# A graph network on one core: in the account of a hand-planned order, the transposed attention squares land later

## The chip, the core and the metric

The kernel runs on one core of a Trainium2 chip. The metric is device time in microseconds for one launch. A profiled execution also gives the span from the first to the last instruction, and a trace of all engines: TensorE (PE, its weight loads PEld), VectorE (DVE), ScalarE (ACT), GpSimd (POOL) and SyncE (SP), which issues the DMAs here.

## What is computed

There are 128 graphs of 128 nodes with 256 features, and a dense adjacency matrix for each. Everything is float32.

```python
# layer 0: gated graph network, three steps with shared GRU weights
h = relu(layernorm(x))
for i in range(3):
    m = h @ weight[i]
    aggr = einsum('bst,bsd->btd', A, m)          # A = adj != 0
    h = gru_cell(aggr, h, w_ih, w_hh, b_ih, b_hh)
x = x + h
# layer 1: graph attention
h = relu(layernorm(x))
Wh = h @ W.T
s1, s2 = Wh @ a1, Wh @ a2
e = leaky_relu(s1[:, :, None] + s2[:, None, :], 0.2)
att = softmax(where(adj == 0, -inf, e), axis=-1)
x = x + einsum('bij,bjo->bio', att, Wh)
```

## The kernel before

**Tiling.** Four graphs form a group (`G = 4`), so there are 32 groups (`NG`). Each group goes through three GRU steps and then through an epilogue, which is the attention layer. The steps of several groups are interleaved by a fixed list, `plan`: 96 steps, and each group's three steps stand apart so that other groups' steps lie between them.

**A GRU step** (`gru_step`) has two phases. Each phase is seven block products in the manner of Strassen's method, and each product is 6 matmuls of 128x256 (L690) into the PSUM tiles `u`, `m7`, `c1` and `c2`; in the profile they are `u`, `m` and `c`. ScalarE and VectorE copy and add these between the products (L710 to L725) and make the gates (L743 to L785). The neighbours' sums for a later step come from the gather `pa` (L598), 16 matmuls of 128x128.

**The epilogue** (`epilogue`) of a group does the following. The state is turned to rows and added to the input (`x1`). The rows are normalised (`norm_scales`, `norm_apply`) into `h_b`. The two score vectors are made by `scalar_tensor_tensor` with a sum (L922). The squares `e`, 128x128 for each graph, are filled from a broadcast score line, masked, reduced and passed through the exponential (L958 to L979). Then the squares have to be transposed. For groups 0 to 28 that is `squares_by_blocks`: VectorE transposes 32x32 blocks into `prT` (L571), and `by_way_of_dram` moves the blocks to their places, with four DMAs to a DRAM tile (`z_e<-prT`) and four back (`e<-z_e`). For the last three groups (`late`) TensorE transposes them through PSUM (`pp`, L988, and `prT`, L992). Then come the attention product `pq<-e,h_b` (`gathered`, L598, 16 matmuls), two copies to `hs` on ScalarE (L1019), the product with W in `po` (L1027), the last addition on VectorE (L1036) and one DMA to the output. The last group's epilogue is cut in two halves of two graphs each.

**PSUM.** `misc` has three banks. `pa` and `pq` take two of them at once, and so do the row transposes of the late groups (`pr_o`, L489) where they handle four graphs; `po`, `pp` and `ps` take one each.

**The order.** The order of instructions on every engine is decided while the program is built. The class `Order` keeps an account of time: `free` holds when each engine is next free, and `rooms` when each buffer is. Each piece of work is a generator that yields what it needs: an engine, a length, the time at which its inputs are ready and perhaps a room. It gets back the time at which the account has it done. `HOP` (0.2) is added to every ready time, and a DMA is taken to have landed `LAND` (2.5) after its issue. A task has a rank: the next step's inputs have 0, state updates 0.5, prologues 1 and epilogues 2. The account only sorts instructions into the queues. On the chip each instruction waits for its own semaphores, whatever the account said.

A gate product counts for 1.3 on TensorE. After each product two things happen: `fill` places work of the other engines up to the product's end, and `matmuls` puts other TensorE work behind it, if the account has it ready by then:

```python
        def matmuls(self, most):
            end = self.free[PE] + most
            ...
                    if engine != PE or self.free[PE] >= end:
                        continue
                    if self.begin(PE, *needs) <= self.free[PE] + 0.05:
                        self.issue(task)
```

So `pq` enters TensorE's queue at the end of the first product at which the account has the squares landed and two `misc` banks free. In `by_way_of_dram` that landing is counted from the end of the block transpose: four issues of 0.67, `LAND`, four issues of 0.42, `LAND`, and whatever else the account has on SyncE.

All DMAs are issued by SyncE in that one order (the helper `dma`, L60). An issue that has to wait there holds up those behind it.

Of the kernel before, what the change touches and what calls it, by code (L numbers as in the profile page):

```python
# [15 lines left out]
D = 256  # L16
C = D // P
G = 4
# [9 lines left out]
def preln_gnn_kernel(  # L28
# [14 lines left out]
    nc = tc.nc  # L43
    B = x.shape[0]
    NG = B // G
# [11 lines left out]
    put = on_pe  # L57
# [107 lines left out]
    PE, ACT, DVE, DVE2, POOL, SP = "PE", "ACT", "DVE", "DVE2", "POOL", "SP"  # L165
# [125 lines left out]
    order = Order()  # L291
# [185 lines left out]
            put(nc.scalar.copy(hT[:, c, :], pt))  # L477
        return hT, t

    def to_rows(hT, ready, name, pairs=range(G // 2)):  # L480

        banks = []
        t = yield PE, 0.44 * len(pairs), ready, "misc", len(pairs)
        for half in pairs:
            pt = order.open("misc", f"pr_{name}_{half}").rearrange("p (k d) -> p k d", d=D)
            for k in range(2):
                for c in range(C):
                    n = half * 2 + k
                    put(nc.tensor.transpose(  # L489
                        pt[:, k, c * P : (c + 1) * P], hT[:, c, n * P : (n + 1) * P], ident  # L490
                    ))
            banks.append(pt)
        return banks, t
# [6 lines left out]
    def by_way_of_dram(tmp, to, n, ready, name, room=None):  # L500

        z = None
        for i in range(Q):
            t = yield SP, SMALL, ready
            if z is None:
                z = dram.tile([32, Q * n, Q, 32], F32, tag=f"z{n}", name=f"z_{name}", bufs=4)
            dma(z[:, :, i, :], tmp[i * 32 : (i + 1) * 32])
        order.close(f"tq_{name}" if n > G else f"prT_{name[:-2]}", t + LAND)
        ready = t + LAND
        rows_ = z.rearrange("r (q n) i a -> q r (n i a)", q=Q)  # L510
        to_ = None
        for q in range(Q):
            t = yield (SP, 0.42, ready) if to_ is not None else (SP, 0.42, ready, room)
            if to_ is None:
                to_ = to()
            dma(to_[q * 32 : (q + 1) * 32], rows_[q])
        return t + LAND
# [49 lines left out]
    def squares_by_blocks(e, prT, ready, name):  # L567

        t = yield DVE, 0.63, ready
        tmp = prT.rearrange("p k s -> p (k s)").rearrange("p (q k a) -> p q k a", q=Q, a=32)  # L570
        put(nc.vector.transpose(  # L571
            tmp.rearrange("p q k a -> p k q a"), e.rearrange("p k (q a) -> p k q a", q=Q)
        ))
        return (yield from by_way_of_dram(
            tmp.rearrange("p q k a -> p (q k) a"), lambda: e.rearrange("p k s -> p (k s)"),
            G, t, f"{name}_e",
        ))

    def rows(s, ready, name):

        banks, ready = yield from to_rows(s.hT, ready, name)
        h = None
        for half, pt in enumerate(banks):
            t = yield (ACT, 0.57, ready) if half else (ACT, 0.57, ready, "h")
            order.close(f"pr_{name}_{half}", t)
            if h is None:
                h = order.open("h", f"h_{name}")
            put(nc.scalar.copy(h[:, half * 2 : half * 2 + 2, :], pt))
        return h, t
# [48 lines left out]
    def state(s, o, old, new, v, z, ready):  # L638

        n = v[:, o, :]  # L640
        t = yield ACT, 0.66, ready
        put(nc.scalar.activation(n, n, AF.Tanh, bias=bih[:, 2 * C + o : 2 * C + o + 1], scale=1.0))  # L642
        s.halves.append(t)
        if len(s.halves) == C:
            n, new_, z_ = flat(v), flat(new), flat(z)
            t = yield DVE2, 1.22, max(s.halves)
            put(nc.vector.tensor_tensor(new_, flat(old), n, ALU.subtract))
            t = yield DVE2, 1.22, t - HOP
            put(nc.vector.scalar_tensor_tensor(new_, z_, 1.0, new_, ALU.add, ALU.mult))
            t = yield DVE2, 1.22, t - HOP  # L650
            put(nc.vector.scalar_tensor_tensor(new_, new_, 0.5, n, ALU.mult, ALU.add))
            s.halves.append(t)
            s.hT, s.aT = new, None
            s.l += 1
            if s.l < NL:
                s.hT_ready = max(s.halves)
                if s.by_blocks():
                    s.rows = order.add(1, state_rows(s))
                if s.due:
                    s.task = order.add(0, inputs(s, s.hT_ready))  # L660
            else:

                pairs = range(G // 2)
                for p in [pairs] if s.g < NG - 1 else [pairs[:1], pairs[1:]]:
                    order.add(2, epilogue(s, p, max(s.halves)))

    def gru_step(s, last):

# [134 lines left out]
    banks = dict.fromkeys(("u", "c1_0", "c1_1", "c2"), 0.0)  # L803
# [66 lines left out]
            "p n t -> p (n t)"  # L870
        ).rearrange("p (k s) -> p k s", s=P)

    def epilogue(s, pairs, ready):

        g = s.g
        graphs = range(2 * pairs[0], 2 * pairs[-1] + 2)
        n = len(graphs)
        part = slice(graphs[0], graphs[-1] + 1)
        cols = slice(part.start * P, part.stop * P)
        name = f"{g}_{pairs[0]}"  # L880
        bank_t, row_t, graph_t = 0.57 * n / G + 0.02, 0.62 * n / G + 0.02, 0.11 * n

        late, h = g >= NG - 3, None

        end = g >= NG - 2
        e_room, hs_room = (None, None) if end else ("e", "hs")
        if late:
            banks, ready = yield from to_rows(s.hT, ready, f"{name}_o", pairs)
        else:
            h, ready = yield from to_rows_by_blocks(s.hT, ready, f"b{name}")  # L890
            s.kept.append(h)
            if g < NG - XT:
                yield from load_x1(s)
                ready = max(ready, s.x1_ready)
        x1 = s.x1
        for half in pairs:
            t = yield (DVE if late else DVE2), 0.62, ready
            k2 = slice(half * 2, half * 2 + 2)
            if late:
                order.close(f"pr_{name}_o_{half}", t)  # L900
                put(nc.vector.tensor_add(x1[:, k2, :], x1[:, k2, :], banks[half - pairs[0]]))
            else:
                put(nc.vector.tensor_add(x1[:, k2, :], x1[:, k2, :], h[:, k2, :]))
        rstd, nb, t = yield from norm_scales(x1, graphs, t - HOP, f"b{name}")
        h, t = yield from norm_apply(
            x1, graphs, rstd, nb, t, f"b{name}", s.kept, "tq" if end else "h"
        )

        v = small.tile([P, 2, G], F32, tag="s", name=f"s_{name}")
        one, two = v[:, 0, :], v[:, 1, :] if late else score_tiles[g % 2][:, 0:G]  # L910
        ready = t
        for i in (1, 0):
            for k in graphs:
                first = not late and s.prT is None
                t = yield (DVE2, 0.53, ready, "prT") if first else (DVE2, 0.53, ready)
                if s.prT is None and late:
                    s.prT = io.tile([P, G, P], F32, tag="at", name=f"prT_{g}", bufs=AT)
                if s.prT is None:
                    s.prT = order.open("prT", f"prT_{g}")

                unused = s.prT[:, part.start : part.start + 2, :].rearrange("p k s -> p (k s)")
                put(nc.vector.scalar_tensor_tensor(  # L922
                    unused, h[:, k, :], 1.0, wa[:, i, :], ALU.mult, ALU.mult,
                    accum_out=(one, two)[i][:, k : k + 1],
                ))
# [8 lines left out]
        else:  # L934
# [4 lines left out]
            ready, line = t, None  # L939
# [62 lines left out]
        ))  # L1002

        banks, ready = yield from gathered(h, prT, t, f"pq_{name}", graphs)
        final = pairs[-1] + 1 == G // 2
        if final:
            order.close(f"h_b{g}_0", ready)
        if final and not end:
# [9 lines left out]
            hs = s.hs  # L1018
            put(nc.scalar.copy(hs[:, c, cols], pq[:, cols]))  # L1019
        ready = t  # L1020
        for half in pairs:
            t = yield PE, 1.73, ready, "misc"
            po = order.open("misc", f"po_{g}_{half}").rearrange("p (k d) -> p k d", d=D)
            for j in range(2):
                k = half * 2 + j
                for c in range(C):
                    put(nc.tensor.matmul(  # L1027
                        po[:, j, :], hs[:, c, k * P : (k + 1) * P], gwt[:, c, :],
                        start=(c == 0), stop=(c == C - 1),
                    ))  # L1030
            if final and half == pairs[-1] and not end:
                order.close(f"hs_{g}", t)
            for j in range(2):
                k = half * 2 + j
                t2 = yield DVE, 0.4, t
                put(nc.vector.scalar_tensor_tensor(  # L1036
                    x1[:, k, :], po[:, j, :], rs[:, k : k + 1], x1[:, k, :], ALU.mult, ALU.add
                ))
            order.close(f"po_{g}_{half}", t2)
        t = yield SP, 0.45, t2  # L1040
        ks = slice(g * G + part.start, g * G + part.stop)
        dma(out[ks].rearrange("b t d -> t b d"), x1[:, part, :])
# [140 lines left out]
```

## Time and profile before

| | |
|---|---|
| median of 3 runs | 2139.47 us (2136.89 to 2141.38) |
| the profiled execution's own time | 2138.47 us |
| its span | 2136.7 us |
| granted TensorE clock, mean | 0.999 |
| busy: PE, PEld | 2119.0 us (99%), 1879.0 us (88%) |
| busy: DVE, ACT, POOL | 1724.6 us (81%), 1302.4 us (61%), 105.9 us (5%) |
| moved by the SyncE queue | 209.87 MB |
| DMA issues `z_e<-prT`, `e<-z_e` | 116 each, 64 KB each |

A busy share is an average over the span. Matmuls are pipelined and their ends are modelled, so consecutive matmuls overlap in the trace; what counts is when the next one starts. "PE pq L598 <- DMA e<-z_e" means that TensorE's instruction at line 598 that writes `pq` waited for the DMA from `z_e` into `e`.

### The profile page before, as it was taken

Reading aid. Unit: us, or ns where it says so; the run is one execution under the profiler, and the core shown is the slowest. Engines: PE = TensorE matmul, PEld = TensorE weight load, DVE = VectorE, ACT = ScalarE, POOL = GpSimd, SP = SyncE. Lnnn points to the kernel's source line nnn. Section 1 sums busy time; section 2 is a strip of 40 time slices with the busy share of each in tenths; the row PEclk is TensorE's granted clock in tenths of the full one; section 3 lists DMA queues with packets and bytes.
Section 4 is the critical chain, followed back from the end, with each engine's and each line's share of the span. In section 5 each row is a group of like instructions: output and inputs, shape, how many; then the busy total and the mean of one; then the engine's idle time right before and its main releaser. Section 6 shows DMA issues by size and latency. Waiting matters only on the chain.

```text
span 2136.7 us, 32121 instructions
## 1 busy us (share of the span) xinstructions
PE 2119.0 (99%) x10763; PEld 1879.0 (88%) x10763; DVE 1724.6 (81%) x3763; ACT 1302.4 (61%) x2855; POOL 105.9 (5%) x204
## 2 busy tenths in 40 slices
PE   9999999999999999999999999999999999999997
PEld 7888888888888888888888888888888888888886
DVE  7777888788888888888888788888878887887777
ACT  6556566566666666665666566556656665665665
POOL 2000000000000000000000000000000000000000
PEclk9999999999999999999999999999999999999999
DMA  5333454444554273544445453734445354443301
GB/s 158 64 85 81 88 118 93 110 102 92 128 110 113 59 166 68 118 94 114 101 88 129 100 123 67 156 73 115 94 109 109 85 129 102 100 94 80 83 26 40
DMA packets 667942, 211.93 MB, mean 99 GB/s; under 512 B 578304, under 2 KB 644608, under 8 KB 667776
## 3 DMA queue, kind: packets, MB, share of 16 engines
q1 hardware_dynamic: 667776, 209.87, 43.9%
q8 instruction: 85, 1.39, 0.3%
q14 instruction: 81, 0.66, 0.1%
HBM read 121.91 MB, written 87.88 MB: 98 GB/s over the span
## 4 chain that ended last, share of the span: by engine, by line
PE 96%; DMA 1%; ACT 1%; DVE 1%; SPq 1%; issue 0%; POOL 0%; DVEq 0%; ACTq 0%; POOLq 0%
PE c L690 34%; PE u L690 34%; PE m L690 11%; PE pa L598 8%; PE po L1027 5%; PE pq L598 3%; PE pw L357 1%; SPq L60 1%; DMA e<-z_e 1%; DMA z_e<-prT 0%; ACT e L979 0%; DMA wih<-in_w_ih_t 0%; ACT v L642 0%; PE pr_o L489 0%; DVE v L785 0%
## 5 line engine op out<-in xcount | busy, mean ns | idle before, releaser
L778 ACT ACTIVATE z<-c,brz 128x256 f32<-128x256 f32 x384 | 185.3, 482 | 300.1 <-PE c L690 155.4
L690 PE MATMUL u<-t_h,s_hh 128*128 128x256 f32 x1152 | 343.3, 380 | 0.5 <-DVE c L716 0.3
L690 PE MATMUL u<-t_a,s_f 128*128 128x256 f32 x1152 | 311.3, 379 | 0.0
L690 PE MATMUL c<-aT,s_f 128*128 128x256 f32 x1152 | 311.3, 379 | 0.0
L743 ACT ACTIVATE r<-c,brz 128x256 f32<-128x256 f32 x384 | 175.6, 478 | 208.4 <-PE c L690 132.0
L716 DVE TENSOR_TENSOR c<-u,m 128x512 f32<-128x512 f32 x192 | 134.0, 698 | 144.9 <-PE u L690 144.7
L690 PEld LDWEIGHTS c<-aT,s_f 128*128 128x128 f32 x1152 | 218.9, 190 | 29.8
L690 PEld LDWEIGHTS u<-t_a,s_f 128*128 128x128 f32 x1152 | 218.9, 190 | 29.8
L690 PEld LDWEIGHTS u<-t_h,s_hh 128*128 128x128 f32 x1152 | 217.3, 190 | 31.5 <-DVE c L716 1.6
L785 DVE TENSOR_TENSOR v<-v,c 128x256 f32<-128x256 f32 x384 | 154.2, 420 | 110.6 <-ACT z L778 57.7
L690 PE MATMUL c<-hT,s_hh 128*128 128x256 f32 x768 | 228.4, 379 | 0.0
L721 ACT COPY c<-u 128x512 f32<-128x512 f32 x192 | 109.4, 570 | 117.3 <-PE u L690 116.9
L713 ACT COPY m<-m 128x512 f32<-128x512 f32 x192 | 112.5, 586 | 112.0 <-PE m L690 112.0
L750 ACT ACTIVATE v<-c,bhn 128x256 f32<-128x256 f32 x384 | 172.3, 477 | 0.0
L690 PE MATMUL m<-t_h,s_hh 128*128 128x256 f32 x576 | 171.5, 379 | 0.0
L690 PE MATMUL c<-t_h,s_hh 128*128 128x256 f32 x576 | 171.3, 379 | 0.0
L690 PEld LDWEIGHTS c<-hT,s_hh 128*128 128x128 f32 x768 | 145.8, 190 | 19.8
L725 DVE TENSOR_TENSOR c<-u,m 128x512 f32<-128x512 f32 x192 | 132.0, 687 | 37.5 <-ACT c L721 36.0
L690 PE MATMUL m<-t_a,s_f 128*128 128x256 f32 x576 | 155.6, 379 | 0.0
L690 PE MATMUL u<-aT,s_f 128*128 128x256 f32 x576 | 155.6, 379 | 0.0
L690 PE MATMUL c<-t_a,s_f 128*128 128x256 f32 x576 | 155.6, 379 | 0.0
L710 ACT COPY c<-u 128x512 f32<-128x512 f32 x192 | 109.5, 570 | 53.3 <-PE u L690 53.3
(125 smaller groups left out, 3900.0 us busy)
## 6 DMA issues: line engine op xcount, KB each, us to landing
z<-tq SPq DMA_DIRECT2D x248, 128.0 KB
h<-z SPq DMA_DIRECT2D x248, 128.0 KB
xt<-in_x SPq DMA_DIRECT2D x31, 512.0 KB
z_a<-tq_a SPq DMA_DIRECT2D x120, 128.0 KB
hT_a<-z_a SPq DMA_DIRECT2D x120, 128.0 KB
z_b<-tq_b SPq DMA_DIRECT2D x116, 128.0 KB
h_b<-z_b SPq DMA_DIRECT2D x116, 128.0 KB
x<-in_x SPq DMA_DIRECT2D x29, 512.0 KB
```

The lines of the kernel that those rows point to most:

```text
L598: put(nc.tensor.matmul(pa[:, k * P : (k + 1) * P], h[:, k, c * P : (c + 1) * P], A[:, k, :], start=True, stop=True,))
L690: put(nc.tensor.matmul(to(q), S[0][:, gate_no, weight, :], moving, start=first and q == 0 and i == 0, stop=(i == len(ends) - 1), skip_grou ...
L710: put(nc.scalar.copy(c1[0], u))
L713: put(nc.scalar.copy(m, m7))
L716: put(nc.vector.tensor_tensor(c2, u, m, ALU.add))
L721: put(nc.scalar.copy(c1[1], u))
L725: put(nc.vector.tensor_tensor(c22, u, m, ALU.add))
L743: put(nc.scalar.activation(r[:, o, cols], src, AF.Tanh, bias=brz[:, o : o + 1], scale=0.5))
L750: put(nc.scalar.activation(v[:, o, cols], src, AF.Identity, bias=bhn[:, o : o + 1], scale=0.5))
L778: put(nc.scalar.activation(z[:, o, cols], src, AF.Tanh, bias=brz[:, C + o : C + o + 1], scale=0.5))
L785: put(nc.vector.tensor_tensor(v[:, o, cols], v[:, o, cols], src, ALU.add))
L1027: put(nc.tensor.matmul(po[:, j, :], hs[:, c, k * P : (k + 1) * P], gwt[:, c, :], start=(c == 0), stop=(c == C - 1),))
```

## The change

`squares_by_blocks` returns a time that is 2.0 us later than before. This time is what the epilogue hands on as the ready time of `gathered`, so in the account the transposed squares have landed 2.0 us later. The functions that took pairs of graphs now take a list of graphs and cut it into twos (`twos`); tile names follow the first graph in place of the pair. The instructions and their number are the same.

```diff
+    def twos(graphs):
+        return [graphs[i : i + 2] for i in range(0, len(graphs), 2)]
+
-    def to_rows(hT, ready, name, pairs=range(G // 2)):
+    def to_rows(hT, ready, name, graphs=range(G)):
         banks = []
-        t = yield PE, 0.44 * len(pairs), ready, "misc", len(pairs)
-        for half in pairs:
+        t = yield PE, 0.22 * len(graphs), ready, "misc", len(twos(graphs))
+        for two in twos(graphs):
...
-        return (yield from by_way_of_dram(
+        t = yield from by_way_of_dram(
             tmp.rearrange("p q k a -> p (q k) a"), lambda: e.rearrange("p k s -> p (k s)"),
             G, t, f"{name}_e",
-        ))
+        )
+        return t + 2.0
...
-                pairs = range(G // 2)
-                for p in [pairs] if s.g < NG - 1 else [pairs[:1], pairs[1:]]:
-                    order.add(2, epilogue(s, p, max(s.halves)))
+                for graphs in [range(G)] if s.g < NG - 1 else [range(2), range(2, 4)]:
+                    order.add(2, epilogue(s, graphs, max(s.halves)))
...
-    def epilogue(s, pairs, ready):
+    def epilogue(s, graphs, ready):
...
-        for half in pairs:
-            t = yield (DVE if late else DVE2), 0.62, ready
-            k2 = slice(half * 2, half * 2 + 2)
+        for i, two in enumerate(twos(graphs)):
+            t = yield (DVE if late else DVE2), 0.31 * len(two), ready
+            k2 = slice(two[0], two[-1] + 1)
...
+        place = min(part.start, G - 2)
...
-                unused = s.prT[:, part.start : part.start + 2, :].rearrange("p k s -> p (k s)")
+                unused = s.prT[:, place : place + 2, :].rearrange("p k s -> p (k s)")
...
-        final = pairs[-1] + 1 == G // 2
+        final = graphs[-1] + 1 == G
...
-        for half in pairs:
-            t = yield PE, 1.73, ready, "misc"
+        for two in twos(graphs):
+            t = yield PE, 0.865 * len(two), ready, "misc"
```

More of the change, by code (lines that the diff above doesn't have):

```diff
@@ L478, in to_columns @@
         return hT, t
-    def to_rows(hT, ready, name, pairs=range(G // 2)):
+    def twos(graphs):
+        return [graphs[i : i + 2] for i in range(0, len(graphs), 2)]
+    def to_rows(hT, ready, name, graphs=range(G)):
         banks = []
-        t = yield PE, 0.44 * len(pairs), ready, "misc", len(pairs)
-        for half in pairs:
-            pt = order.open("misc", f"pr_{name}_{half}").rearrange("p (k d) -> p k d", d=D)
-            for k in range(2):
+        t = yield PE, 0.22 * len(graphs), ready, "misc", len(twos(graphs))
+        for two in twos(graphs):
+            pt = order.open("misc", f"pr_{name}_{two[0]}").rearrange("p (k d) -> p k d", d=D)
+            for k, n in enumerate(two):
                 for c in range(C):
-                    n = half * 2 + k
                     put(nc.tensor.transpose(
@@ L584, in rows @@
             t = yield (ACT, 0.57, ready) if half else (ACT, 0.57, ready, "h")
-            order.close(f"pr_{name}_{half}", t)
+            order.close(f"pr_{name}_{2 * half}", t)
             if h is None:
@@ L871, in place_of_e @@
         ).rearrange("p (k s) -> p k s", s=P)
-    def epilogue(s, pairs, ready):
+    def epilogue(s, graphs, ready):
         g = s.g
-        graphs = range(2 * pairs[0], 2 * pairs[-1] + 2)
         n = len(graphs)
@@ L879, in epilogue @@
         cols = slice(part.start * P, part.stop * P)
-        name = f"{g}_{pairs[0]}"
+        name = f"{g}_{graphs[0]}"
         bank_t, row_t, graph_t = 0.57 * n / G + 0.02, 0.62 * n / G + 0.02, 0.11 * n
@@ L887, in epilogue @@
         if late:
-            banks, ready = yield from to_rows(s.hT, ready, f"{name}_o", pairs)
+            banks, ready = yield from to_rows(s.hT, ready, f"{name}_o", graphs)
         else:
@@ L895, in epilogue @@
         x1 = s.x1
-        for half in pairs:
-            t = yield (DVE if late else DVE2), 0.62, ready
-            k2 = slice(half * 2, half * 2 + 2)
+        for i, two in enumerate(twos(graphs)):
+            t = yield (DVE if late else DVE2), 0.31 * len(two), ready
+            k2 = slice(two[0], two[-1] + 1)
             if late:
-                order.close(f"pr_{name}_o_{half}", t)
-                put(nc.vector.tensor_add(x1[:, k2, :], x1[:, k2, :], banks[half - pairs[0]]))
+                order.close(f"pr_{name}_o_{two[0]}", t)
+                put(nc.vector.tensor_add(
+                    x1[:, k2, :], x1[:, k2, :], banks[i][:, 0 : len(two), :]
+                ))
             else:
@@ L1020, in epilogue @@
         ready = t
-        for half in pairs:
-            t = yield PE, 1.73, ready, "misc"
-            po = order.open("misc", f"po_{g}_{half}").rearrange("p (k d) -> p k d", d=D)
-            for j in range(2):
-                k = half * 2 + j
+        for two in twos(graphs):
+            t = yield PE, 0.865 * len(two), ready, "misc"
+            po = order.open("misc", f"po_{g}_{two[0]}").rearrange("p (k d) -> p k d", d=D)
+            for j, k in enumerate(two):
                 for c in range(C):
@@ L1030, in epilogue @@
                     ))
-            if final and half == pairs[-1] and not end:
+            if final and two[-1] == graphs[-1] and not end:
                 order.close(f"hs_{g}", t)
-            for j in range(2):
-                k = half * 2 + j
+            for j, k in enumerate(two):
                 t2 = yield DVE, 0.4, t
@@ L1038, in epilogue @@
                 ))
-            order.close(f"po_{g}_{half}", t2)
+            order.close(f"po_{g}_{two[0]}", t2)
         t = yield SP, 0.45, t2
```

## The prediction

> **What bounds the kernel now.** I read the head of the page first, then what TensorE waits for, then the chain of waits and the timeline around the longest of those waits, and last the end of the run.
>
> ```profile
> span 2136.7 us, 32121 instructions
> PE 2119.0 (99%) x10763; PEld 1879.0 (88%) x10763; DVE 1724.6 (81%) x3763; ACT 1302.4 (61%) x2855; POOL 105.9 (5%) x204
> ```
>
> TensorE issues without a break, so only two things can shorten the run: TensorE work taken away, which this change does not do, or TensorE's idle time, 2136.7 - 2119.0 = 17.7 us in all. The waits of the PE queue say where the part that this change can touch lies:
>
> ```profile
> PE pp L988 <- ACT e L979: 4.3, 3, 2.7
> PE pq L598 <- DMA e<-z_e: 3.0, 4, 1.8
> PE pq L598 <- ACT prT L992: 2.3, 4, 0.7
> PE pw L357 <- DMA wih<-in_w_ih_t: 1.6, 2, 1.2
> ```
>
> Columns: idle us in total, times, longest. The first and third lines are the last three groups (after 2101 us), the fourth the start. The second is ours: TensorE is at `pq`, the attention product, and the transposed squares `e` have not come back from DRAM. The chain of waits in the stretch 380 to 396 us shows what made the longest of them late (start, us, what):
>
> ```profile
> 381.31 0.56 SPq L60
> ...
> 383.49 2.21 DMA z_e<-prT
> ...
> 387.07 2.45 DMA e<-z_e
> 389.52 0.14 issue
> 389.66 2.02 PE pq L598 x16
> 391.68 2.59 PE c L690 x12
> ```
>
> The two landings took 2.21 and 2.45 us, as the order assumes (LAND = 2.5). What the order has too early is the queue: in the timeline of SyncE the vector transpose of the squares ended at 377.35 us, but four other transfers (`h<-z`) and their wait stand first, and a 512 KB load stands between the two halves:
>
> ```profile
> 378.14 3.12 SPq L60 DMA_DIRECT2D h<-z  x4
> 381.31 2.79 SPq L60 DMA_DIRECT2D z_e<-prT  x4
> 384.16 0.61 SPq L60 DMA_DIRECT2D x<-in_x  x1
> 385.78 1.71 SPq L60 DMA_DIRECT2D e<-z_e  x4
> ```
>
> And on TensorE there (idle time before it in brackets):
>
> ```profile
> 387.26 0.59 PE L690 MATMUL u<-t_h,s_hh 128*128 128x256 f32 x2
> 389.66 0.57 PE L598 MATMUL pq<-e,h_b 128*128 128x128 f32 x3 [1.81 <-DMA e<-z_e]
> ```
>
> **What the wait costs.** Matmul ends are modelled, so I take starts: in a gapless stretch one 128x256 matmul follows another after 0.216 us. From the last gate matmul to the first `pq` it is 2.19 us here (389.66 - 387.47), and 0.70, 0.69, 0.53 and 0.96 us near 780, 976, 1171 and 1367 us. All other 24 block-transposed groups show 0.216. The loss is 5.07 - 5 x 0.216 = 3.99 us. The weight loader's own line for it (5.1 us in 5) is the upper bound, since it runs ahead of the array; 3.99 is what the array loses, and I take that.
>
> These five groups, and 574, 1551 and 1746 us where `e` comes just in time, are every third group: 39 us after the one before. In that phase the `h<-z` transfers meet the squares on the queue.
>
> **The change part by part.** (1) The rewriting from pairs to lists of graphs keeps every instruction: the costs are the same numbers (0.22 x 4 = 0.44 x 2, 0.31 x 2 = 0.62, 0.865 x 2 = 1.73), the split of the last group is the same (graphs 0-1 and 2-3), and `place` equals `part.start` for the starts that occur, 0 and 2. Names alone differ. Cost 0.
>
> (2) `return t + 2.0`: for 29 of the 32 groups (the last three transpose on TensorE), `pq` counts as ready 2.0 us later. Nothing is removed or added; `pq` (16 matmuls, 1.75 us) goes behind more gate products. TensorE takes such work only at a product's end, and a product is 6 matmuls, 6 x 0.216 = 1.30 us. So 2.0 us is one boundary or two, 1.30 or 2.59 us, where `pq` went as soon as it was ready, and may be none where something else held it (the groups whose transpose ends 13.5 us before `pq`, against 10.1 to 10.4 elsewhere). In the tight phase the wait is what is left of 1.97, 0.49, 0.47, 0.31, 0.74 us after that: two boundaries leave 0, one leaves 1.97 - 1.30 = 0.67 us in one group. Gain 3.3 to 3.99 us; I take 3.99, since 2.0 us crosses two boundaries in (2.0 - 1.3)/1.3 = 54% of the positions.
>
> What moves with it: two `hs` copies on ScalarE (0.59 us each), 16 `po` matmuls (3.46 us), four 0.43 us VectorE updates, one output transfer on SyncE, and the release of `e`, `h_b` and `hs`. All of it is later by at most 2.59 us. In the tight phase it costs nothing, because the copies already stand 6 us behind `pq` (near 584 us: `pq` ends at 586.4, `hs` starts at 592.9), so they need not move at all; without that cover the output is 2.6 us later, which nobody reads. `pq` holds two of the three `misc` PSUM banks until the copies; the next `pa`, which needs two, comes 8.3 us after `pq` in the second phase (749.3 against 741.1) and 20 us after in the tight one. `pa` feeds a step that starts some 12 products later, a cover of 15 us. What is late next in the tight phase: nothing on this page, since the next idle time of TensorE in the steady part is 0.3 us on VectorE (`u` behind `c` L716).
>
> (3) The end. Group 28's `pq` (2083 us) moves too, and with it the row transposes of group 30 (`pr_o`, two banks) and the scores of 29. After the last gate product, 2101.3 us, the run is one dependency chain:
>
> ```profile
> 2100.26 1.03 PE L690 MATMUL c<-aT,s_f 128*128 128x256 f32 x4
> ...
> 2103.97 1.48 PE L988 MATMUL pp<-ident,e 128*128 128x128 f32 x4 [2.68 <-ACT e L979]
> 2106.13 3.60 PE L598 MATMUL pq<-prT,h_b 128*128 128x128 f32 x16 [0.68 <-ACT prT L992]
> ...
> 2117.86 2.05 PE L598 MATMUL pq<-prT,h_b 128*128 128x128 f32 x16 [0.67 <-ACT prT L992]
> ```
>
> The same 16 matmuls take 3.60 us after the idle stretch and 2.05 us later; the granted clock over 2101 to 2137 us is 0.95, over the run 0.999. A rearranged end can lose that drop (-1.55 us) or slip by what `pr_o` slips (+2.6 us). Group 29's squares are reduced at 2099.0 and its exponentials wait for ScalarE until 2103.4, so 4.4 us of slack cover a later group 29; group 30's scores have less. I take 0 with both ends.
>
> **A rule against the change.** The landings of one tight group took 2.35 and 2.92 us, of another 2.21 and 2.45. The Trainium skill, "DMA: Bandwidth & Descriptors", in its part on the two cost components, gives a transfer a fixed cost of some 2.0 us and a small rest by size; by that the order's 2.5 us would be generous, no wait would be there and the change would be worth 0. The rows differ: 2.92 us is over 2.5, and the queue adds its own lateness.
>
> **The sum.** The profiled execution took 2138.47 us (span 2136.70 and 1.77 around it): 2138.47 - 3.99 + 0 = 2134.5. The median of the runs is 2139.47, 1.0 above it; they spread from 2136.89 to 2141.38, 4.5 us. In the steady part the wait on `e<-z_e` is TensorE's only wait on a transfer, and so the only place where I see runs differ by the state of the queues. So I take the spread to be in this wait: it goes too, all runs come to 2134.5, 4.97 us (0.23%) below the median.
>
> A measurement of this kernel can tell about 0.2% from no change, 4.3 us.
>
> **The rivals.** *Within 0.2%* (36%): the spread lies elsewhere. Then the median falls by 3.3 to 3.99 us, to 2135.5 or 2136.2, and with a slip of 2.6 us at the end to 2138.1 or 2138.8. For it: the fastest run, 2136.89, is only 1.6 us under the profiled one. Against it: no other wait on a transfer is shown. That `pq` does not move at all in the tight phase is excluded, 2.0 us being more than one product. That the five waits come from longer delays than two products is also excluded by 1.97 < 2.59.
>
> *Slower* (7%): the end. Group 28's `pq` keeps two `misc` banks when group 30 needs two; its row transposes go behind the `hs` copies and `po`, and groups 30 and 31 run one after the other on the last chain. A slip there counts in full, because nothing is left to fill TensorE; it needs 4.0 us to cancel the gain and 8.3 us to be slower by 0.2%. As prices: `pr_o` late by one `pq` and two `po` (1.75 + 3.46 = 5.2 us), and a second 1.55 us from the clock and one exponential group of 1.64 us moved behind: 8.4 us, net +4.4 us, 2143.9. Against it: the slack of 4.4 us at group 29, and a slip that starts at 2.6 us.
>
> **How the numbers follow.** Forecast, faster by over 0.2%: 57%, 2134.5 us. Low end: the forecast less the clock drop of 1.55 us and 0.9 us for a run like the fastest one, 2132.0. High end: the second case with one boundary and the slip, 2138.8. Left out are the slower case and some of both ends.
>
> **What would show it.** Right: the PE queue's line `pq <- DMA e<-z_e` is gone or under 0.5 us; in the groups near 376, 574, 768 us the transpose-to-`pq` distance grows by 1.3 or 2.6 us, and the gate product after `pq` is no longer the one that follows now; PE busy stays at 2119 us; the span is near 2132.7 us; chain shares of `e<-z_e` fall to nothing. The step on the median is wrong if runs of the changed kernel still spread by 4 us. Wrong altogether: `pq` waits on the transfer still, or a new line of over 1 us (`pa` or `u` behind ScalarE), or the stretch after the last gate product is longer than 35.4 us.

## The result, and the profile after

The changed kernel is slower: 2144.67 us median (2142.53 to 2147.05) against 2138.52 us for the kernel before in the same set of runs (2136.89 to 2141.38), a ratio of 1.0025 with a 95% interval of 1.0017 to 1.0033. The forecast was 2134.5 us. In the later sets the kernel before ran at 2141.1 to 2141.8 us, so every ratio below is to the runs of its own set. (A ratio is the record's estimate from all runs of a set; it can differ from the ratio of the two medians by 0.0004.)

The head of the page after:

```profile
span 2140.4 us, 32101 instructions
PE 2118.0 (99%) x10763; PEld 1878.9 (88%) x10763; DVE 1725.1 (81%) x3763; ACT 1302.0 (61%) x2855; POOL 104.2 (5%) x204
```

The work is the same. The waits of the PE queue (total us, times, longest):

```profile
PE pq L602 <- DMA e<-z_e: 5.3, 6, 1.3
...
PE pp L993 <- ACT e L984: 3.4, 2, 2.9
...
PE po L1031 <- ACT hs L1024: 2.3, 1, 2.3
...
PE pr_o L492 <- DVE hT L655: 1.8, 1, 1.8
```

The wait that should have gone is larger, and two waits of the end are new. By starts, as in the prediction, the loss is 6.3 us in six groups (7, 10, ... 22) in place of 4.0 in five. The groups fall into three phases, each of them every third group. In the order of before, groups 2, 5, ... 23 are the tight ones, whose squares meet the `h<-z` transfers on the queue, and groups 1, 4, ... 22 are what the prediction calls the second phase. In the new order groups 7, 10, ... 22 are the tight ones, and groups 5, 8, ... 23 have no wait. The timeline of SyncE at the worst of them, group 16, whose block transpose ended at 1287.50 us:

```profile
1280.58 3.23 SPq L60 DMA_DIRECT2D z_a<-tq_a  x4
1283.85 3.44 SPq L60 DMA_DIRECT2D z<-tq  x4
1287.45 2.36 SPq L60 DMA_DIRECT2D hT_a<-z_a  x4
1289.91 0.39 SPq L60 DMA_DIRECT2D out<-x  x1
1290.35 0.50 SPq L60 DMA_DIRECT2D h_b<-z_b  x1
1290.96 2.28 SPq L60 DMA_DIRECT2D h<-z  x4
1293.34 3.57 SPq L60 DMA_DIRECT2D z_e<-prT  x4
1296.96 0.62 SPq L60 DMA_DIRECT2D x<-in_x  x1
1298.72 1.70 SPq L60 DMA_DIRECT2D e<-z_e  x4
```

The squares now stand behind `hT_a`, an output, `h_b` and `h`, and leave 5.8 us after their transpose (5.2 to 6.3 us in the waiting groups; 1.6 to 4.0 us in the waiting groups before). So `pq`, 2.0 us later in the account, waits for squares that are late by more than they were.

Where the orders part is seen first in the second phase, in group 1. ScalarE before:

```profile
352.80 0.59 ACT L440 ACTIVATE h_a<-xt,norm_a 128x256 f32<-128x256 f32 x1
353.67 0.57 ACT L721 COPY c<-u 128x512 f32<-128x512 f32 x1 [0.27 <-PE u L690]
354.15 0.59 ACT L1019 COPY hs<-pq 128x512 f32<-128x512 f32 x1
```

ScalarE after:

```profile
352.95 0.60 ACT L440 ACTIVATE h_a<-xt,norm_a 128x256 f32<-128x256 f32 x1
353.80 0.51 ACT L781 ACTIVATE z<-c,brz 128x256 f32<-128x256 f32 x1 [0.24 <-DVE c L728]
...
359.37 0.57 ACT L1024 COPY hs<-pq 128x512 f32<-128x512 f32 x1
```

TensorE before, then after:

```profile
349.09 1.95 PE L598 MATMUL pq<-e,h_b 128*128 128x128 f32 x16
357.35 1.95 PE L598 MATMUL pa<-A,h 128*128 128x128 f32 x16
```

```profile
349.19 1.95 PE L602 MATMUL pq<-e,h_b 128*128 128x128 f32 x16
361.33 1.95 PE L602 MATMUL pa<-A,h 128*128 128x128 f32 x16
```

`pq` is one product later in the order (its time hardly moves, because this run began its products 1.0 us earlier). That is enough for its first copy to `hs` to miss its slot behind the activations of the prologue and come 10 us after `pq` in place of 5. Until then two of the three `misc` banks are taken, and the next gather `pa`, which needs two, goes from 8.3 to 12.1 us after `pq`. TensorE does not stop for that. But behind it the rest is sorted anew: some 1,500 rows differ between the listings of the two orders, which have some 10,000 rows each (a row is a run of like instructions without line numbers; a moved one counts twice; all such counts here are rounded, since they go by what is taken as alike). With 0.0 in place of 2.0 no row differs, so the rewriting to lists of graphs does nothing.

**The end.** In the new order `pp` and `pq` of group 29 stand ahead of the last gate products, 2.2 us of TensorE work. What follows the last gate product takes 35.7 us all the same (35.6 before). The chain of waits shows why: it now runs through VectorE, which has scores and three state updates to do in a row.

```profile
2106.68 0.43 DVE prT L927 x2
2107.12 1.24 DVE hT L651
2108.38 1.24 DVE hT L653
2109.64 1.22 DVE hT L655
2110.86 0.79 DVE xt L1039 x2
2111.65 0.35 DVE prT L927 x2
```

**Where the span's 3.7 us are.** The first gate product starts 1.0 us earlier (16.0 against 17.1 us; it differs from run to run); waits for `e` cost 2.3 us more; group 29's two pieces cost 2.2 us ahead of the last gate product, of which the end gives nothing back. -1.0 + 2.3 + 2.2 + 0.1 = 3.6 us. This accounts for the two profiled runs. The one after is the fastest of its set, and the 6.2 us between the medians hold more than was profiled here.

### The profile page after: what moved, and what is told of

Read it like the earlier page. It is cut to its first block, busy times and chain, and to the rows that moved or that the text cites. A ratio compares the mean times of both kernels' runs of the same rounds, so it can differ in the third digit from the quotient of the medians.

```text
span 2140.4 us, 32101 instructions
## 1 busy us (share of the span) xinstructions
PE 2118.0 (99%) x10763; PEld 1878.9 (88%) x10763; DVE 1725.1 (81%) x3763; ACT 1302.0 (61%) x2855; POOL 104.2 (5%) x204
## 5 line engine op out<-in xcount | busy, mean ns | idle before, releaser
L724 ACT COPY c<-u 128x512 f32<-128x512 f32 x192 | 109.4, 570 | 123.6 <-PE u L693 123.2
L640 DVE SCALAR_TENSOR_TENSOR v<-r,v 128x1024 f32<-128x1024 f32 x96 | 117.4, 1223 | 21.3 <-ACT v L753 19.6
```

The lines of the kernel that those rows point to most:

```text
L640: put(nc.vector.scalar_tensor_tensor(flat(v), flat(r), 1.0, flat(v), ALU.add, ALU.mult))
L724: put(nc.scalar.copy(c1[1], u))
```

## The experiments

The table has the profiles of all runs. "Waits" is the sum of the late starts of `pq<-e`; a late start is the time from the start before to the first `pq`, less 0.216 us. "End" is from the end of the last gate product to the end of the span, where that end is the last start plus 0.216 us (the prediction went by the modelled end, 2101.3 us, and so had 35.4 us before).

| run | ratio to before, 95% | span | waits | last gate product ends | end |
|---|---|---|---|---|---|
| before | 1 | 2136.7 | 4.0 | 2101.1 | 35.6 |
| after | 1.0025 (1.0017 to 1.0033) | 2140.4 | 6.3 | 2104.7 | 35.7 |
| moved_pq_alone | 0.9967 (0.9955 to 0.9980) | 2132.7 | 0 | 2097.0 | 35.7 |
| changed_moved_pq | 0.9982 (0.9973 to 0.9991) | 2134.5 | 0.3 | 2098.9 | 35.5 |
| groups_before_24 | 1.0024 (1.0015 to 1.0033) | 2146.1 | 6.9 | 2108.0 | 38.1 |
| groups_from_24 | 1.0010 (1.0002 to 1.0019) | 2140.8 | 4.1 | 2102.9 | 37.8 |
| changed_again | 1.0020 (1.0011 to 1.0029) | 2141.7 | 6.5 | 2106.0 | 35.7 |
| changed_z_on_gpsimd | 1.0007 (0.9998 to 1.0016) | 2141.0 | 1.8 | 2105.4 | 35.7 |
| changed_warm_end | 1.0015 (1.0006 to 1.0023) | 2143.9 | 7.4 | 2107.6 | 36.3 |
| moved_pq_warm_end | 0.9971 (0.9959 to 0.9982) | 2132.1 | 0 | 2096.0 | 36.2 |
| tight_groups_only | 0.9974 (0.9965 to 0.9984) | 2131.9 | 0 | 2096.3 | 35.6 |
| second_phase_only | 1.0161 (1.0145 to 1.0177) | 2172.5 | 26.3 | 2135.4 | 37.1 |
| one_us_later | 0.9980 (0.9971 to 0.9989) | 2133.6 | 1.5 | 2098.2 | 35.4 |
| dearer_issues | 0.9985 (0.9976 to 0.9994) | 2135.7 | 0 | 2097.3 | 38.4 |

**1. Only `pq` moved, in the order of before.** The matmuls of `pq` are kept in a list and written two products later; the account knows nothing of it. (The program has 8 of them, which the profile shows as the 16 rows that are called 16 matmuls here and in the prediction.) The rows of the two orders differ in these matmuls alone.

```diff
...
-        banks, ready = yield from gathered(h, prT, t, f"pq_{name}", graphs)
+        behind = 2 if g in range(2, 24, 3) else 0
+        banks, ready = yield from gathered(h, prT, t, f"pq_{name}", graphs, behind)
...
```

> The order of the kernel before, with nothing else changed than this: in the eight tight groups (2, 5, ... 23) the 16 matmuls of pq stand two gate products (2.59 us) later on TensorE. Theory 'the order' (the later pq takes the wait away, and the loss of the change comes from the rest of the order, which was sorted anew): the wait on e<-z_e goes, the time falls by 3.99 us, to about 2134.5 us, and TensorE has no new idle time. Rival 'a later pq does harm' (the copies to hs, po and the PSUM banks follow it): no gain, or slower by 1 us or more.

The span is 2132.7 us, 4.0 us under the kernel before, and its median 2134.74 us. The timeline of TensorE at the first tight group has no idle time before `pq`:

```profile
389.37 0.59 PE L696 MATMUL c<-aT,s_f 128*128 128x256 f32 x2
389.80 0.59 PE L696 MATMUL c<-hT,s_hh 128*128 128x256 f32 x2
390.24 1.95 PE L597 MATMUL pq<-e,h_b 128*128 128x128 f32 x16
```

So the price of the wait was right, and a `pq` two products later harms nothing. What the prediction had wrong is that the rest stays. (The fall of the medians, 7.1 us, is more than the 4.0 of the spans; the profile of the kernel before is of a run of the first set, and what its slower runs of this set hold was not profiled.)

**2. The same in the order after**, with `g in range(4, 24, 3)`.

> The order of the changed kernel, with nothing else changed than this: in the tight groups of its order (4, 7, ... 22) the 16 matmuls of pq stand two gate products (2.59 us) later. Theory 'the order': the wait, 6.3 us in six groups in its trace, goes, and the time falls from 2144.7 to 2138.4 us. Rival 'the end' (the whole loss lies after the last gate product, and the waits are hidden): the time stays at 2144.7 us.

The waits fall from 6.3 to 0.3 us and the span by 5.9 us. 2137.43 us is 0.18% under the kernel before. So the waits are not hidden, and the rival that all the loss lies in the end falls.

**3. and 4. The change for part of the groups.**

```diff
-        return t + 2.0
+        return t + (2.0 if int(name) < 24 else 0.0)
```

> The changed kernel with the 2.0 for groups 0 to 23 alone, so that the last five block-transposed groups return the old time. Theory 'the order' (the loss is a larger wait in the tight groups, 6.3 us against 4.0, and a worse end): the waits of the changed kernel stay, +2.3 us, and the end is a third one, between that of the two kernels: 2139 to 2145 us. Rival 'the end': as fast as the kernel before, 2138.5 us within 1 us.

```diff
-        return t + 2.0
+        return t + (2.0 if int(name) >= 24 else 0.0)
```

> The changed kernel with the 2.0 for groups 24 to 28 alone. Theory 'the order': the order up to 1838 us and its 4.0 us of wait are those of the kernel before, and only the end differs, by at most the 2.4 us that it is worse in the changed kernel's trace: 2137 to 2141 us. Rival 'the end': the full loss, 2144.7 us.

Both are slower than before, and both have a third kind of end, 38.1 and 37.8 us. The steady part has the waits of the changed kernel in the first (6.9 us) and those of before in the second (4.1 us), as 'the order' expects. Both medians, 2146.92 and 2143.68 us, lie over their ranges: the ends are longer than expected, and the kernel before ran 3.3 us slower in this set than in the set from which the ranges were taken. The two do not add up to the change, since each end is another order.

**5. The changed kernel again.**

> The changed kernel once more, beside the others of this set on one chip, for a second profile. Theory 'the order': 0.25% slower than the kernel before, with waits on e<-z_e of about 6 us in the groups 7, 10, ... 22 and a stretch after the last gate product of 35 to 36 us. If the spread of its runs (2142.5 to 2147.1 us) lies in these waits or in the clock of the end, one of the two differs from the first profile by the difference in time.

The waits are 6.5 us, and there is one that the first profile lacks: 1.6 us at 908 us, where `u` waits for VectorE. VectorE itself had stood still for a transfer (timeline of SyncE, then of VectorE):

```profile
895.43 2.47 SPq L60 DMA_DIRECT2D hT_a<-z_a  x4
```

```profile
902.43 0.76 DVE L458 TENSOR_TENSOR t_h<-hT_a 128x256 f32<-128x256 f32 x2 [2.13 <-DMA hT_a<-z_a]
```

VectorE goes on 4.5 us after the last of these issues, against 2.4 to 2.7 us in the other tight groups of this run: the transfer was late to land, not late to be issued. So a transfer can hold up TensorE in a second way, through VectorE, which depends on the run. The kernel before has no such wait of VectorE for `hT_a`.

**6. The squares on another queue.** In the order after, GpSimd issues the first four transfers.

```diff
-            dma(z[:, :, i, :], tmp[i * 32 : (i + 1) * 32])
+            if n > G:
+                dma(z[:, :, i, :], tmp[i * 32 : (i + 1) * 32])
+            else:
+                put(nc.gpsimd.dma_start(z[:, :, i, :], tmp[i * 32 : (i + 1) * 32]))
```

> The order of the changed kernel, with the four z_e<-prT transfers of each group issued by GpSimd in place of SyncE. Theory 'the queue' (the tight groups' squares are late because they stand behind other transfers on SyncE, 5.8 to 7.0 us after their block transpose): the wait of pq falls from 6.3 us to under 1 us, and the time by 5 to 6 us. Rival 'the trip' (the way through DRAM is itself longer than the order's account): the waits stay, and the time stays at 2144.7 us.

In the tight groups they start 0.3 us after the transpose in place of 5.2 to 6.3, and the waits for `e` fall from 6.3 to 1.8 us. That speaks for the queue, not the trip, but less clearly than it looks. The way back, `e<-z_e`, is still on SyncE behind `h<-z` and a load, and starts 8.0 to 10.1 us after the transpose in place of 9.9 to 11.2. And in part the waits are only moved: TensorE stands at `u` a few products ahead of `pq`. The ratio is 1.0007 against 1.0020 in the fifth experiment, with intervals that overlap, because the other wait grows (waits of the PE queue, then the timeline of VectorE):

```profile
PE u L696 <- DVE c L722: 5.3, 5, 2.3
...
PE pq L605 <- DMA e<-z_e: 1.5, 1, 1.5
```

```profile
1491.61 0.76 DVE L458 TENSOR_TENSOR t_h<-hT_a 128x256 f32<-128x256 f32 x2 [3.00 <-DMA hT_a<-z_a]
```

The squares' transfers now run while `hT_a` is on its way, and VectorE has `hT_a` 2.8 to 4.3 us after its last issue, in place of 2.3 to 2.8. Whether the one slows the other is not shown; no run separates it.

**7. and 8. Extra matmuls at the end**, against the clock drop; the second is on top of the first experiment, with `g == 29`.

```diff
             pp = order.open("misc", f"pp_{name}")
+            for _ in range(20 if g == 30 else 0):
+                put(nc.tensor.matmul(pp[:, 0:P], ident, ident, start=True, stop=True))
```

> The changed kernel with 20 extra 128x128 matmuls (some 2.2 us, their result is overwritten) ahead of the pp transposes of group 30, where TensorE is idle for 2.94 us, so that the clock drop of 6.8 us there may go. Theory 'clock' (the worse end is the longer clock drop): pq of group 30 takes about 2.0 us in place of 3.78 and the time falls by 1.7 us or more. Rival 'chain' (VectorE and ScalarE set the end): no change within 1 us.

> The order of the kernel before with pq two products later in the tight groups (the first experiment), and 20 extra 128x128 matmuls ahead of the pp transposes of group 29, where TensorE is idle for 2.68 us. Theory 'clock': the drop goes, pq of group 29 takes 2.05 us in place of 3.60, and the time is 1.5 us under that of the first experiment. Rival 'chain': the same time as the first experiment.

Neither settles it. The 20 matmuls took 4.6 to 4.7 us, twice what I had reckoned, and so delayed `pp`. `pq` behind them did run in 2.05 us, but the drop came elsewhere (a granted clock of 0.66 over 2110 to 2115 us in the second), and the ends are 0.5 to 0.6 us longer. The second is level with the first experiment, 0.9971 against 0.9967.

**9. and 10. Which groups do the harm.** With `2.0 if int(name) in range(2, 24, 3) else 0.0`, the tight groups alone:

> The changed kernel with the 2.0 for the eight tight groups 2, 5, ... 23 alone. Theory 'banks' (the harm comes from the second-phase groups 1, 4, ... 22: their later pq misses the slot of its first copy to hs on ScalarE, keeps two of three misc banks 5 us longer and pushes the next gather pa, and with it everything behind): with those groups left alone the order stays nearly that of the kernel before, the 4.0 us of wait go, and the time falls by 3 to 5 us (ratio 0.998). Rival 'any change of the account re-sorts the order to no good': same as the changed kernel, 0.2% slower than before.

and with `range(1, 24, 3)`, the second phase alone:

> The changed kernel with the 2.0 for the groups 1, 4, ... 22 alone, which in the kernel before had no wait. Theory 'banks': these alone re-sort the order; the copies to hs come 10 us after pq in place of 5, waits on e<-z_e or on VectorE of 4 us and more are there, and the time is 0.1 to 0.3% above the kernel before. Rival 'the re-sorting is chance': within 0.1% of the kernel before, or faster.

This is the clearest pair. The tight groups alone: some 100 rows of the order differ, no wait is left, 0.26% faster than before. The second-phase groups alone, which had no wait: some 1,000 rows differ and the kernel is 1.6% slower, 34 us, five times what I expected. In that run the copies come 10.2 us behind `pq` and `pa` 12.1 us, as the theory has it. (The third phase alone, groups 0, 3, ... 21, was not run: with the 2.0 for these, the program builds the order of before, and no row differs.) The waits of the second-phase run lie in the groups 5, 8, ... 23, which are not delayed in it: their squares leave SyncE 5.0 to 6.5 us after the transpose, in place of 1.4 to 2.8 before, and the waits are 3.3 to 4.7 us each (waits of the PE queue):

```profile
PE pq L602 <- DMA e<-z_e: 25.2, 7, 4.5
```

At six of the seven waits the clock drops as well. One of the six, as timeline of TensorE and by stretch (the granted clock is the third number from the end):

```profile
1389.42 3.75 PE L602 MATMUL pq<-e,h_b 128*128 128x128 f32 x16 [4.52 <-DMA e<-z_e]
```

```profile
1380.00:1389.00 9.00, 4.91 (x28) 4.09 (x26) 8.62 (x23) 4.45 (x9) 1.69 (x3) 0.89 0.82 199
1389.00:1394.00 5.00, 4.58 (x19) 4.44 (x20) 0.49 (x1) 0.00 (x0) 0.00 (x0) 0.52 0.00 0
```

`pq` takes 3.75 us there and 1.95 at full clock. At the seventh the clock stayed at 1.00:

```profile
1589.82 2.02 PE L602 MATMUL pq<-e,h_b 128*128 128x128 f32 x16 [3.10 <-DMA e<-z_e]
```

The page's PE time is 2131.3 us in place of 2119.0, so the drops cost some 12 us, and the waits 22 us more than before: 34 us. In the changed kernel the same pattern comes in other groups, and its tight groups have the 2.0 us too: there the waits stay at 0.7 to 1.5 us, and the clock at 1.00.

**11. A smaller constant**, `return t + 1.0`.

> The changed kernel with 1.0 in place of 2.0. Theory 'banks': 1.0 is too little to move the second-phase groups past the slot of their copies, so the order stays, while pq of the tight groups goes one product (1.30 us) later. Of the waits 1.97, 0.49, 0.47, 0.31, 0.74 only 0.67 us is left: 3.3 us faster than the kernel before (ratio 0.9985), give or take 1 us for the end, which moves too. Rival 'a constant there does harm whatever its size': slower than before by some 0.1%.

0.20% faster. Some 60 rows differ, and the second phase keeps its order: there `pq` starts 10.6 us after the transpose, as before, and in the tight groups one product later. The waits left are 0.5 and 1.0 us, more than the 0.67 expected.

**12. Another entry of the account**, in the kernel before: `SMALL = 0.8` in place of 0.67.

> The kernel before with the account's price of one 64 or 128 KB issue on SyncE raised from 0.67 to 0.80 (the trace has 0.64 to 0.86 for one), and nothing added to the landing. Theory 'the queue' (the account's SyncE runs ahead of the real one): the waits on e<-z_e fall from 4.0 to under 2 us; the time falls by 2 us unless the new order loses it elsewhere. Rival 'the trip': the waits stay at 4 us.

No wait on `e<-z_e` is left, with nothing added to the landing, and the last gate product ends 3.8 us earlier, 0.8 of it by an earlier start. The end gives 2.8 us of it back (waits of the PE queue):

```profile
PE pp L988 <- ACT e L979: 6.9, 1, 6.9
PE pr_o L489 <- DVE hT L651: 3.0, 1, 3.0
```

Six versions are faster than the kernel before. The three fastest are the first experiment (0.9967), the eighth on top of it (0.9971) and the ninth (0.9974); their intervals overlap.

## Why the prediction was wrong, step by step

*The wait and its price* were right for the profiled run. Measured by starts, 3.99 us; with `pq` alone moved, the span fell by 4.0 us, and the end stayed as long.

*"Two boundaries leave 0"* was right for the order of before and wrong for the one that came. In the trace after, the tight groups' squares leave SyncE 5.2 to 6.3 us after their transpose, and 0.7 to 1.5 us of wait are left in six groups behind a `pq` that was moved.

*"What moves with it ... costs nothing"* is the step that failed. I had the second phase in hand, the two banks and the `pa` 8.3 us behind `pq`, and asked only whether `pa` could make TensorE wait; its cover of 15 us was enough, and TensorE did not wait for it. What I did not ask is what a later `pa` does to the queues. I also gave the copies of the tight groups as the case for all: there they stand 6 us behind `pq` and need not move, but in the second phase the first one stood in a slot 3.1 us behind `pq` (354.15 against 351.04), and missed it. The ninth, tenth and eleventh experiments show that moving this phase does the harm; that it goes by the banks is read from the traces and the order's rule, and no run isolates it. In place of nothing, the new order cost 2.3 us more of wait and 2.2 us at the end.

*The end* was taken as 0 with bounds of -1.55 and +2.6 us. In the profile it cost 2.2 us, inside the bounds, by another way than the rival's: group 29 moved ahead of the last gate product, and VectorE became the chain. The rival "slower" had named the end alone, and 8.3 us for it; in the profiled runs the loss from the first gate product on is smaller, and half of it lies in the wait.

*The spread.* I took the whole spread of the runs to be in the wait on `e<-z_e`. The first experiment has no such wait, and its runs still spread from 2133.43 to 2137.52 us, so not all of it lies there. Some may: the first, eighth and ninth experiments, without a wait on `e<-z_e`, have standard deviations of 0.9 to 1.4 us against 1.7 to 1.9 for the kernel before in their sets, and their medians are lower by 5.6 to 7.1 us, more than the wait of the profiled run. No profile of a slower run of the kernel before was taken, so what its waits are stays open.

*Excluded too soon:* that the waits "come from longer delays than two products" was excluded by 1.97 < 2.59, which holds for the old order only.

*The rule on the cost of a DMA* was not what decided. The lateness of the squares is in the issue queue: on another queue they left 0.3 us after their transpose. The Trainium skill, "DMA: Bandwidth & Descriptors", gives the 2.0 us that the prediction cites for transfers that GpSimd issues. Those of both kernels here are issued by SyncE, and the landings that the prediction shows took 2.21 to 2.92 us; in the sixth experiment, where GpSimd issues the squares, the median from issue to landing is 2.4 us.

*Smaller readings*, on which nothing rests: in the tight phase `pa` comes 18.3 us behind `pq`, not 20, and `pq` starts 13.7 us after the transpose in the groups that something else holds and 10.3 to 10.6 us in those without a wait, not 13.5 and 10.1 to 10.4.

*The clock* was no part of the sum for the steady part, and the changed kernel loses nothing by it there. The Trainium skill, "TensorE: Matmul & The Clock Gate", in its part on the clock gate, has the clock fall to half after an idle window of some 3.4 us. The runs agree roughly. The wait of 2.0 us in the kernel before left the granted clock at 1.00 (380 to 400 us). In the tenth experiment the five waits of 3.5 to 4.7 us brought it down to 0.50, and of the two of 3.3 us one did (985 us) and one did not (1590 us).

## What to carry to other kernels

Where a program sorts its own instructions, a constant in its account is not a delay but a new order: compare the two orders row by row before pricing the edit, and price what moves in every group, not in the group that has the wait. To take a known wait away, move the waiting work alone, or the account's entry for the groups that wait: both gained some 0.3% here where the constant for all lost 0.25%. When work that holds a shared buffer moves, look for the slot in which its reader was to free that buffer, and for who wants the buffer next.

## What the runs showed of the hardware

A wait of 3.3 to 4.7 us on TensorE can cost more than its length: in the tenth experiment 7 of them took 26.3 us, and the half-clock stretches at six of them some 12 us of matmul time. A float32 matmul shows as two matmul rows in these profiles: the 20 extra ones of 128x128 as 40 rows and 4.6 us, the 8 of a `pq` as 16, the 3 of a gate product as 6. A transpose of 128x128 against the identity shows as one.
